# Two-slot self-attention: small copies on ScalarE, the norms of two slots together, half products and row sums in another order

## The chip, the core and the metric

One core of a Trainium2 chip runs the kernel. Its engines are TensorE (PE: matmuls; PEld: its weight loads), VectorE (DVE), ScalarE (ACT), GpSimd (POOL) and SyncE (SP), which here only issues transfers. Each engine works through its own queue in order and waits on semaphores for the others. The metric is the time of the whole program on the device, in microseconds (us); lower is better. The profile is one execution under the hardware profiler.

## What is computed

A decoder block in float32 on `x` of shape (8, 224, 512): self-attention, cross-attention against a context of 750 tokens, and a quantised feed-forward part, each followed by a residual add and a layernorm. The change touches the self-attention alone:

```python
x = _rmsnorm(tokens, norm_w)
q = x @ Wq
k, v = jnp.split(x @ Wkv, 2, axis=-1)
q = _head_rmsnorm(q, q_gamma)       # 16 heads of 64
k = _head_rmsnorm(k, k_gamma)       # x / max(norm, 1e-12) * (gamma + 1) * 8
sim = jnp.einsum('bhid,bhjd->bhij', q, k)
sim = jnp.tanh(sim / 50.0) * 50.0 * 64 ** -0.5
attn = jax.nn.softmax(sim, axis=-1)
out = jnp.einsum('bhij,bhjd->bhid', attn, v)
x = _layernorm(tokens + merge_heads(out) @ Wo)
```

## The kernel before

**Slots and groups.** Two batches `u` and two heads `j` form one *slot*. Four pairs of batches (groups 0 to 3) times eight pairs of heads (`hp` 0 to 7) make 32 slots, `m` = 0 to 31, `g, hp = divmod(m, 8)`. The order of every compute engine's instructions is the order of the program text (a manual schedule); only SP's transfers are placed by the framework.

**One slot.** `self_scores(m)` multiplies keys and queries on PE into `sc_a` (16 matmuls); ACT takes tanh and then exp into `pr`, with keys on the partitions. `self_values(m)` multiplies `pr` with the values (16 matmuls into `ov_a`), and DVE scales by the inverse row sums `rc_a` into `oT`. A slot's values are computed one slot later, in slot m + 1. In even groups POOL copies the end of `oT` into `oT_tail`. `inverse_sums(m)` makes `rc_a`: DVE transposes and adds 32 by 32 blocks of `pr` (L508, into `sm_q`), three copies bring the four quarters of the partitions together (L517), L521 adds them, two reciprocals follow (L527), three copies spread the result (L531), and two transposes broadcast it (L538).

**Two slots' queries and keys.** In an even slot `project_pair` computes queries and keys of slots m + 2 and m + 3 by a scheme with seven half products instead of eight. Each is eight matmuls and goes into one of two PSUM tiles, `mx` and `mz`, where they accumulate: ACT copies `mx` away after each of its products, DVE adds `mz` to the copy after each of its own (`add`, L397). A tile may be written again only when that copy or add has read it. The function is a generator: its yields place its parts between the other work of the slot. ACT squares the results (L393, `sq_qk`).

**Norms.** `head_norms` is called in odd slots for the two next slots, one after the other: DVE adds the squares in 32 by 32 blocks (L428, `nm_q`), four copies fetch the other half of each head (L435, `nm_o`), then an add, a maximum (L438, L439), and on POOL the power -0.5 (`rsqrt`, L129, into `nm_i`). `scale_qk` (L446, L451) transposes the inverse norms over the old squares and scales queries and keys with them; `self_scores` needs this.

**What else a slot carries.** `project_v` multiplies a tile of 128 tokens with the value weights (8 matmuls of 512 columns, copied to `v` by ACT, L471); in groups 0 to 2 `transpose_xn` and `copy_xn` turn the next group's normalised tokens, which `scale_x` (L254) makes in the slot before; `square` and `rms_norms` prepare these in slots with `hp` = 0. `self_output` multiplies a finished tile of the group before with `Wo` (16 matmuls of 512 columns, or pairs over half of the rows), in the slots that `out_at` lists, and adds it to `x` on DVE (L588); the layernorm of that tile is started in the next slot (`layernorm`, with its power on POOL) and its scaling (L152) runs at that slot's end. PSUM has three shared tiles for `mx`, `mz`, values, transposes and outputs, two for scores and one for `ov_a`.

Of the kernel before, what the change touches and what calls it, by code (L numbers as in the profile page):

```python
# [38 lines left out]
P = 128  # L39
# [23 lines left out]
def decoder_block(ctx: ExitStack, tc: tile.TileContext, a: dict, out: bass.AP):  # L63
# [153 lines left out]
    with tc.tile_pool(name="a_sb", bufs=2) as sb, tc.tile_pool(  # L217
# [16 lines left out]
        trs, mms, loaded = {}, {}, {}  # L234
        xn, qk, sq_qk, inv, v, oT, rcs = {}, {}, {}, {}, {}, {}, {}
# [35 lines left out]
        def open_qk(m):  # L271

            qk[m] = sb.tile([P, 2, 2, S], F32, name="qk", bufs=4)
            sq_qk[m] = sb.tile([P, 2, 2, S], F32, name="sq_qk")
# [5 lines left out]
        def block_qk(m, w, cols):  # L280
# [3 lines left out]
            if (w, c0) == (0, 0):  # L284
                open_qk(m)
# [79 lines left out]
        def project_pair(j):  # L365
# [4 lines left out]
            open_qk(m + 1)  # L370
# [3 lines left out]
            yield  # L374
# [27 lines left out]
            product(mz, True, 1, b21)  # L402
            add(m, 0)
            yield
            product(mx, False, 4, t2)
            nc.scalar.copy(qk[m][:, 1], mx)
            square_qk(m, 0)
            product(mz, True, 3, t1)
            product(mx, False, 5, t3)
            nc.scalar.copy(qk[m + 1][:, 1], mx)  # L410
            yield
            add(m + 1, 1)
            yield
# [9 lines left out]
        def head_norms(m):  # L423
# [3 lines left out]
            quarter = sb.tile([P, 4 * NB], F32, name="nm_q")  # L427
            nc.vector.tensor_reduce(  # L428
                quarter, sq_qk[m].rearrange("p u w (b c) -> p (u w b) c", c=Q32), AX.X,
                ALU.add, apply_transpose=True,  # L430
            )
            other = sb.tile([P, 4 * NB], F32, name="nm_o", bufs=1)
            for q in range(P // Q32):
                o = q ^ 1
                nc.vector.tensor_copy(  # L435
                    other[q * Q32 : (q + 1) * Q32], quarter[o * Q32 : (o + 1) * Q32]
                )
            nc.vector.tensor_tensor(quarter, quarter, other, ALU.add)  # L438
            nc.vector.tensor_scalar(quarter, quarter, 1e-24, None, ALU.max)  # L439
            inv[m] = sb.tile([P, 2, 2 * NB, 1], F32, name="nm_i")  # L440
            rsqrt(inv[m].rearrange("p u b o -> p (u b o)"), quarter)
# [14 lines left out]
        def project_v(i, c):  # L456

            mm = ps_mm.tile([P, 512], F32, tag="mm", name="mm_v")
# [9 lines left out]
            for b, kt, row, at, n in key_pieces(i):  # L468
                if (b, c) not in v:
                    v[b, c] = sb.tile([P, NT, 512], F32, name="v", bufs=6)  # L470
                nc.scalar.copy(v[b, c][row : row + n, kt, :], mm[at : at + n, :])  # L471
# [31 lines left out]
        def inverse_sums(m):  # L503


            quarter = sb.tile([P, 2, 2, NB, NT, P // Q32], F32, name="sm_q", bufs=1)
            for u in range(2):
# [4 lines left out]
                )  # L512

# [848 lines left out]
```

## Time and profile before

| | us |
|---|---|
| runs of the kernel, median of 3 | 1715.62 (1715.25 to 1716.76) |
| profiled execution, whole | 1714.79 |
| its span, first to last instruction | 1713.0 |
| first scores of the self-attention | 46.7 |
| last values of the self-attention | 521.2 |
| first matmul of the cross-attention's keys | 541.2 |

Durations in the self-attention, mean or median of one instruction, as the groups and tiles of the trace show them:

| instruction | ns |
|---|---|
| L508, row sums of a batch, DVE | 1089 |
| L428, norms of a slot, DVE | 1103 |
| L435 copy of 32 x 28, DVE | 210 (167 to 1083) |
| L517 copy of 32 x 56, DVE | 232 (203 to 1084) |
| L531 copy of 32 x 14, DVE | 167 |
| L438 add, L439 maximum, 128 x 28, DVE | 204, 180 |
| L129 power on 128 x 28, POOL | 4797 |
| L446 transpose, L451 scaling, 128 x 448, DVE | 619, 734 |
| L397 add, L559 `oT`, 128 x 448, DVE | 623, 619 |
| L493 tanh, L499 exp, 128 x 448, ACT | 537, 575 |
| L401 copy of `mx`, L393 square, 128 x 448, ACT | 531, 583 |

A row of the timeline gives the start, the time until the last of the merged instructions ended, the engine, the line, the operation and the tiles; in brackets how long the engine was idle before it and what released it. In a table of stretches each engine has its busy time and, in brackets, its instructions. Matmuls overlap, so a row of eight is longer than the distance to the next row; the distance is what counts.

### The profile page before, as it was taken

The numbers are of one execution on the slowest core, as the hardware profiler recorded it, in microseconds if no ns is written. First come the engines' busy times: TensorE is split into PE (matmuls) and PEld (weight loads), VectorE is DVE, ScalarE is ACT, GpSimd is POOL, SyncE is SP. The second block draws the span as 40 slices with busy tenths as digits, with TensorE's granted clock in tenths as the row PEclk, the third lists the DMA queues.
The fourth block names the chain that finished last, engine by engine and source line by source line (L and its number), as shares of the span: only waits on it lengthen the run. The fifth ranks groups of instructions, "written<-read, shape, count | busy, mean of one in ns | idle before, by whom it ended". The sixth has DMA issues, their size and how long they took to land.

```text
span 1713.0 us, 24297 instructions
## 1 busy us (share of the span) xinstructions
PE 1669.5 (97%) x8962; PEld 1150.1 (67%) x8962; DVE 1291.0 (75%) x2833; ACT 871.9 (51%) x1492; POOL 661.0 (39%) x543
## 2 busy tenths in 40 slices
PE   8999999998989999999999999999999999999998
PEld 5666666675745777776776776777776776774443
DVE  3797888777883776776886886797875776886877
ACT  3555536444531665554564565565443543445663
POOL 3562442432420444344344244344443343443244
PEclk9999999999999999999999999999999999999999
DMA  7143112111212122201121121100000000031434
GB/s 258 50 135 106 43 56 74 53 55 66 93 64 104 58 74 94 74 25 65 44 68 64 44 68 65 38 19 34 1 26 6 4 24 6 1 142 28 76 82 105
DMA packets 85573, 106.72 MB, mean 62 GB/s; under 512 B 38352, under 2 KB 58832, under 8 KB 82512
## 3 DMA queue, kind: packets, MB, share of 16 engines
q1 hardware_dynamic: 85456, 105.19, 19.4%
q8 instruction: 70, 1.15, 0.3%
q14 instruction: 47, 0.39, 0.1%
HBM read 82.36 MB, written 14.16 MB: 56 GB/s over the span
## 4 chain that ended last, share of the span: by engine, by line
PE 87%; DVE 11%; DMA 1%; issue 1%; ACT 0%; POOL 0%; POOLq 0%; SPq 0%; DVEq 0%
PE mm_k L897 15%; PE mm_v L885 15%; PE sc_c L934 9%; PE ov_c L1028 9%; PE mm_q L910 6%; PE mm_co L194 6%; PE mm_f L1163 5%; PE mm_o L579 5%; PE mm_x L383 4%; PE mm_z L383 4%; PE mm_v L461 3%; PE sc_a L483 2%; PE dn L1251 2%; DVE sm_q L508 2%; PE ov_a L551 2%; DVE nm_q L428 1%
## 5 line engine op out<-in xcount | busy, mean ns | idle before, releaser
L1018 POOL TENSOR_TENSOR csh<-cpT 125x672 f32<-125x672 f32 x128 | 207.3, 1619 | 578.8 <-DVE cpT L1008 536.8
L1016 ACT ACTIVATE cpT<-cpT 125x1344 f32<-125x1344 f32 x128 | 169.5, 1325 | 228.6 <-DVE cpT L1008 219.8
L897 PE MATMUL mm_k<-cT,xattn_Wk 128*128 128x375 f32 x768 | 258.6, 486 | 1.7 <-DMA cT<-ctxT 1.7
L885 PE MATMUL mm_v<-xattn_Wv,cT 128*125 128x256 f32 x1152 | 259.1, 379 | 0.0
L885 PEld LDWEIGHTS mm_v<-xattn_Wv,cT 128*125 128x125 f32 x1152 | 216.2, 188 | 28.9
L942 ACT COPY cpT<-sc_c 125x448 f32<-125x448 f32 x384 | 173.7, 560 | 104.3 <-PE sc_c L934 104.2
L897 PEld LDWEIGHTS mm_k<-cT,xattn_Wk 128*128 128x128 f32 x768 | 140.0, 189 | 101.6 <-issue 12.5
L1008 DVE TENSOR_TENSOR cpT<-cpT,mx_b 125x1344 f32<-125x1344 f32 x128 | 193.2, 1550 | 2.2
L129 POOL TENSOR_TENSOR nm_i<-nm_q,mhalf 128x28 f32<-128x28 f32 x32 | 153.0, 4807 | 100.9 <-DVE nm_q L439 100.9
L944 DVE TENSOR_TENSOR cm<-sc_c,cpT 125x448 f32<-125x448 f32 x128 | 74.0, 620 | 146.8 <-ACT cpT L942 146.8
L934 PE MATMUL sc_c<-cqT,ckT 64*125 64x224 f32 x1536 | 163.0, 358 | 0.0
L1028 PE MATMUL ov_c<-cpT,cv 125*64 125x224 f32 x1536 | 159.4, 357 | 0.0
L934 PEld LDWEIGHTS sc_c<-cqT,ckT 64*125 64x125 f32 x1536 | 140.3, 184 | 24.7 <-ACT ckT L904 15.0
L1028 PEld LDWEIGHTS ov_c<-cpT,cv 125*64 125x64 f32 x1536 | 104.6, 137 | 47.3 <-issue 18.2
L904 ACT COPY ckT<-mm_k 128x375 f32<-128x375 f32 x128 | 59.2, 462 | 126.5 <-PE mm_k L897 126.5
L910 PEld LDWEIGHTS mm_q<-xT,xattn_Wq 128*128 128x128 f32 x512 | 96.7, 189 | 16.3
L910 PE MATMUL mm_q<-xT,xattn_Wq 128*128 128x224 f32 x512 | 107.1, 352 | 0.0
L461 PE MATMUL mm_v<-wv,xnT 128*128 128x512 f32 x224 | 101.4, 597 | 0.0
L1163 PE MATMUL mm_f<-ternary,xqT 128*128 128x512 bf16 x448 | 98.7, 379 | 0.9 <-DVE x L1055 0.9
L579 PE MATMUL mm_o<-attn_Wo,oT 128*128 128x512 f32 (+1 forms) x224 | 99.2, 596 | 0.0
L194 PE MATMUL mm_co<-xattn_Wo,coT 128*128 128x512 f32 (+1 forms) x256 | 98.1, 594 | 0.0
L1019 POOL TENSOR_TENSOR csm<-csh 125x224 f32<-125x224 f32 x128 | 93.8, 732 | 10.0
(187 smaller groups left out, 2658.6 us busy)
## 6 DMA issues: line engine op xcount, KB each, us to landing
w_pair<-w_sums_all SPq DMA_DIRECT2D x24, 512.0 KB, 4.3
cT<-ctxT SPq DMA_DIRECT2D x8, 1125.0 KB, 5.6
w_stage<-w_gateT SPq DMA_DIRECT2D x8, 1024.0 KB, 5.2
w_stage<-w_upT SPq DMA_DIRECT2D x8, 1024.0 KB, 5.2
w_stage<-w_downT SPq DMA_DIRECT2D x8, 1024.0 KB, 5.3
tern<-w_t SPq DMA_DIRECT2D x24, 256.0 KB, 2.1
ternary<-tern SPq DMA_DIRECT2D x3, 2048.0 KB, 12.4
w_pair<-attn_Wq SPq DMA_DIRECT2D x36, 128.0 KB, 2.3
```

The source lines that it names most:

```text
L194: nc.tensor.matmul(mm[row : row + m, :], lhsT=oT[:, k, at : at + m], rhs=w[:, k, :], start=(k == 0), stop=(k == NPAIR - 1),)
L579: nc.tensor.matmul(mm[row : row + lhsT.shape[-1], :], lhsT=lhsT, rhs=wo[:, hp, :], start=(hp == 0), stop=(hp == NPAIR - 1),)
L885: nc.tensor.matmul(mm[:, i, :], lhsT=cT[:, k, c * CT : (c + 1) * CT], rhs=xwv[:, k, g * VN : (g + 1) * VN], start=(k == 0), stop=(k == KC ...
L897: nc.tensor.matmul(mm, lhsT=xwk[:, k, hp * P : (hp + 1) * P], rhs=cT[:, k, c * HALF : (c + 1) * HALF], start=(k == 0), stop=(k == KC - 1),)
L910: nc.tensor.matmul(mm, lhsT=xwq[:, k, hp * P : (hp + 1) * P], rhs=xT[:, k, :], start=(k == 0), stop=(k == KD - 1),)
L934: nc.tensor.matmul(sc[j][:, i, :], lhsT=kT[h0 : h0 + DH, ct * CT : (ct + 1) * CT], rhs=qT[h0 : h0 + DH, :], start=True, stop=True,)
L942: nc.scalar.copy(pT[:, j, 2 * c2 : 2 * c2 + 2, :], sc[j])
L1008: nc.vector.tensor_tensor(pT[:, j], pT[:, j], nm[:CT, j] .rearrange("p (o q) -> p o q", o=1) .to_broadcast([CT, NCT, S]), ALU.add,)
L1016: nc.scalar.activation(pT[:, j], pT[:, j], AF.Exp)
L1018: nc.gpsimd.tensor_tensor(half, pT[:, j, 0:3], pT[:, j, 3:6], ALU.add)
L1028: nc.tensor.matmul(ov[h0 : h0 + DH, :], lhsT=v[:, ct, hq * DH : (hq + 1) * DH], rhs=pT[:, j, ct, :], start=(ct == 0), stop=(ct == NCT - 1),)
L1163: nc.tensor.matmul(mm, lhsT=xqTs[i][:, k, :], rhs=w[:, k, cols], start=(k == 0), stop=(k == KD - 1),)
```

## The change

Four things change, all in the self-attention:

- The small copies of norms (L435) and row sums (L517, L531) move from DVE to ACT; the add and the maximum of the norms (L438, L439) move to POOL. The two reciprocals L527 become one.
- The squares of two slots lie in one tile, `sq_pair`, and `head_norms` takes both slots at once (only at the start one at a time). It is now a generator: reduction and copies stand at the end of the even slot, after that slot's own squares; POOL's part stands in the odd slot after `self_values`, ahead of that slot's layernorm.
- `inverse_sums` is a generator too: the reduction stays at the end of its slot; its later parts stand there as well in an even slot (but for the last transposes, which stand ahead of the next `self_values`), and in the next slot, between the parts of `project_pair`, after an odd one.
- The order on PE: the third half product moves ahead of `self_values`; the product with `t1` moves behind `self_scores`; `transpose_xn` moves ahead of `project_v`. In even slots the copy of the values and `copy_xn` come after the sums. Group 3 makes the outputs of group 2 in slots with `hp` 5, 6, 7 instead of 4, 5, 6, and `oT` has 15 buffers instead of 14.

```diff
...
+        sq_pair = sb.tile([P, 2, 2, 2, S], F32, name="sq_qk", bufs=1)
...
         def open_qk(m):
-            qk[m] = sb.tile([P, 2, 2, S], F32, name="qk", bufs=4)
-            sq_qk[m] = sb.tile([P, 2, 2, S], F32, name="sq_qk")
+            for i in range(2):
+                qk[m + i] = sb.tile([P, 2, 2, S], F32, name="qk", bufs=4)
+                sq_qk[m + i] = sq_pair[:, i]
...
             open_qk(m)
-            open_qk(m + 1)
             w = blocks(j)
             b11, _, b21, b22 = input_blocks(j // (NPAIR // 2))
             t1, t2, t3, t4 = (sums_x[:, i] for i in range(4))
-            yield
             mx = ps_mm.tile([P, 2, S], F32, tag="mm", name="mm_x")
             mz = ps_mm.tile([P, 2, S], F32, tag="mm", name="mm_z")
...
             product(mx, True, 0, b11)
             nc.scalar.copy(qk[m][:, 0], mx)
             product(mz, True, 1, b21)
+            yield
             add(m, 0)
             yield
             product(mx, False, 4, t2)
             nc.scalar.copy(qk[m][:, 1], mx)
+            yield
             square_qk(m, 0)
-            product(mz, True, 3, t1)
+            yield
             product(mx, False, 5, t3)
             nc.scalar.copy(qk[m + 1][:, 1], mx)
             yield
+            product(mz, True, 3, t1)
             add(m + 1, 1)
-            yield
             product(mx, False, 2, t4)
             nc.scalar.copy(qk[m + 1][:, 0], mx)
             square_qk(m + 1, 1)
...
             square_qk(m, 1)
             yield
-        def head_norms(m):
-            quarter = sb.tile([P, 4 * NB], F32, name="nm_q")
+        def head_norms(m, i0, i1):
+            quarter = sb.tile([P, 2, 4 * NB], F32, name="nm_q")[:, i0:i1]
+            quarter = quarter.rearrange("p n b -> p (n b)")
             nc.vector.tensor_reduce(
-                quarter, sq_qk[m].rearrange("p u w (b c) -> p (u w b) c", c=Q32), AX.X,
-                ALU.add, apply_transpose=True,
-            )
-            other = sb.tile([P, 4 * NB], F32, name="nm_o", bufs=1)
+                quarter,
+                sq_pair[:, i0:i1].rearrange("p n u w (b c) -> p (n u w b) c", c=Q32),
+                AX.X, ALU.add, apply_transpose=True,
+            )
+            yield
+            other = sb.tile([P, 2, 4 * NB], F32, name="nm_o", bufs=1)[:, i0:i1]
+            other = other.rearrange("p n b -> p (n b)")
             for q in range(P // Q32):
                 o = q ^ 1
-                nc.vector.tensor_copy(
+                nc.scalar.copy(
                     other[q * Q32 : (q + 1) * Q32], quarter[o * Q32 : (o + 1) * Q32]
                 )
-            nc.vector.tensor_tensor(quarter, quarter, other, ALU.add)
-            nc.vector.tensor_scalar(quarter, quarter, 1e-24, None, ALU.max)
-            inv[m] = sb.tile([P, 2, 2 * NB, 1], F32, name="nm_i")
-            rsqrt(inv[m].rearrange("p u b o -> p (u b o)"), quarter)
+            yield
+            nc.gpsimd.tensor_tensor(quarter, quarter, other, ALU.add)
+            nc.gpsimd.tensor_scalar(quarter, quarter, 1e-24, None, ALU.max)
+            for i in range(i0, i1):
+                inv[m + i] = sb.tile([P, 2, 2 * NB, 1], F32, name="nm_i")
+                at = (i - i0) * 4 * NB
+                rsqrt(
+                    inv[m + i].rearrange("p u b o -> p (u b o)"),
+                    quarter[:, at : at + 4 * NB],
+                )
+            yield
         def scale_qk(m):
             rb, r = sq_qk.pop(m), inv.pop(m)
...
                 )
         def project_v(i, c):
             mm = ps_mm.tile([P, 512], F32, tag="mm", name="mm_v")
             at = i * P % (2 * G)
...
                     start=(k == 0),
                     stop=(k == KD - 1),
                 )
-            for b, kt, row, at, n in key_pieces(i):
-                if (b, c) not in v:
-                    v[b, c] = sb.tile([P, NT, 512], F32, name="v", bufs=6)
-                nc.scalar.copy(v[b, c][row : row + n, kt, :], mm[at : at + n, :])
+            def copy_v():
+                for b, kt, row, at, n in key_pieces(i):
+                    if (b, c) not in v:
+                        v[b, c] = sb.tile([P, NT, 512], F32, name="v", bufs=6)
+                    nc.scalar.copy(v[b, c][row : row + n, kt, :], mm[at : at + n, :])
+            return copy_v
         def self_scores(m):
...
         def inverse_sums(m):
             quarter = sb.tile([P, 2, 2, NB, NT, P // Q32], F32, name="sm_q", bufs=1)
             for u in range(2):
                 nc.vector.tensor_reduce(
...
                     prs[u].rearrange("p j t (b c) -> p j t b c", c=Q32),
                     AX.X, ALU.add, apply_transpose=True,
                 )
+            yield
             flat = quarter.rearrange("p u j b t g -> p (u j b t) g")
             for g in range(1, P // Q32):
-                nc.vector.tensor_copy(
-                    flat[:Q32, :, g], flat[g * Q32 : (g + 1) * Q32, :, 0]
-                )
+                nc.scalar.copy(flat[:Q32, :, g], flat[g * Q32 : (g + 1) * Q32, :, 0])
+            yield
             tot = sb.tile([Q32, 2, 2, NB], F32, name="sm_t", bufs=1)
             nc.vector.tensor_reduce(
                 tot.rearrange("p u j b -> p (u j b)"),
                 quarter[:Q32].rearrange("p u j b t g -> p (u j b) (t g)"), AX.X, ALU.add,
             )
             isum = sb.tile([P, 2, 2 * NB, 1], F32, name="sm_i", bufs=1)
-            for j in range(2):
-                nc.vector.reciprocal(
-                    isum[:Q32, j, :, 0].rearrange("p (u b) -> p u b", u=2), tot[:, :, j]
-                )
+            nc.vector.reciprocal(
+                isum[:Q32, :, :, 0].rearrange("p j (u b) -> p j u b", u=2),
+                tot.rearrange("p u j b -> p j u b"),
+            )
+            yield
             for g in range(1, P // Q32):
-                nc.vector.tensor_copy(
+                nc.scalar.copy(
                     isum[g * Q32 : (g + 1) * Q32, g // 2, :, 0],
                     isum[:Q32, g // 2, :, 0],
                 )
+            yield
             rcs[m] = sb.tile([P, 2, S], F32, name="rc_a", bufs=1)
             for j in range(2):
                 half = slice(j * DH, (j + 1) * DH)
...
                     rcs[m][half].rearrange("p u q -> p (u q)"),
                     isum[half, j].to_broadcast([DH, 2 * NB, Q32]),
                 )
+            yield
         def self_values(m):
             g, hp = divmod(m, NPAIR)
...
                             start=(kt == 0),
                             stop=(kt == NT - 1),
                         )
-            oT[m] = sb.tile([P, 2, S], F32, name="oT", bufs=14)
+            oT[m] = sb.tile([P, 2, S], F32, name="oT", bufs=15)
             nc.vector.tensor_tensor(oT[m], ov[:, :, :S], rcs.pop(m), ALU.mult)
             if g % 2 == 0:
...
+        open_qk(0)
...
         nc.vector.tensor_scalar(gscale, gam, 1.0, DH**0.5, ALU.add, ALU.mult)
-        head_norms(0)
-        project_v(0, 0)
-        project_v(1, 0)
+        for _ in head_norms(0, 0, 1):
+            pass
+        project_v(0, 0)()
+        project_v(1, 0)()
         project_qk(1)
         sum_input(0, nc.vector)
         scale_qk(0)
         sum_weights(1, nc.vector)
-        head_norms(1)
+        for _ in head_norms(0, 1, 2):
+            pass
         for i in opened[0][2:]:
-            project_v(i, 0)
-        out_at = [(), (1, 3, 5), (1, 3, 5, 6), (4, 5, 6)]
+            project_v(i, 0)()
+        out_at = [(), (1, 3, 5), (1, 3, 5, 6), (5, 6, 7)]
+        nothing = iter(lambda: None, 0)
+        sums = norms = nothing
         for m in range(NS):
             g, hp = divmod(m, NPAIR)
             even = m % 2 == 0
-            pair = project_pair(m // 2 + 1) if even and m + 2 < NS else None
-            step = (lambda: next(pair)) if pair else (lambda: None)
-            step()
-            step()
-            if even and m > 0:
-                scale_qk(m)
+            c = 1 - hp // 4
+            tiles = opened[g + hp // 4] if g + hp // 4 < NG else ()
+            ahead = opened[g + 1] if g + 1 < NG else ()
+            turned = ahead[hp - 1] if 1 <= hp < 1 + len(ahead) else None
+            pair = nothing
+            if even and m + 2 < NS:
+                pair = project_pair(m // 2 + 1)
+            if even:
+                next(pair)
+                next(sums)
+                if m > 0:
+                    scale_qk(m)
+                next(pair)
+                next(sums)
+                next(pair)
+                next(sums)
+                next(pair)
+            next(sums)
             if m > 0:
                 self_values(m - 1)
-            step()
+            next(norms)
+            next(pair)
             self_scores(m)
             for i in due:
                 scales.append(layernorm([i]))
             due.clear()
             if even:
                 scale_qk(m + 1)
-            elif m + 1 < NS:
-                head_norms(m + 1)
-                head_norms(m + 2)
-            step()
-            step()
-            inverse_sums(m)
-            c = 1 - hp // 4
-            tiles = opened[g + hp // 4] if g + hp // 4 < NG else ()
+            next(pair)
+            if turned is not None:
+                transpose_xn(turned)
+                if not even:
+                    copy_xn(turned)
+            copy_v = lambda: None
             if hp % 4 < len(tiles):
-                project_v(tiles[hp % 4], c)
+                copy_v = project_v(tiles[hp % 4], c)
+            if not even:
+                copy_v()
+            sums = inverse_sums(m)
+            next(sums)
+            norms = nothing
+            if even:
+                if pair is not nothing:
+                    norms = head_norms(m + 2, 0, 2)
+                next(norms)
+                next(sums)
+                copy_v()
+                next(norms)
+                next(sums)
+                next(sums)
+                if turned is not None:
+                    copy_xn(turned)
             for f in scales:
                 f()
             scales.clear()
-            ahead = opened[g + 1] if g + 1 < NG else ()
-            if 1 <= hp < 1 + len(ahead):
-                transpose_xn(ahead[hp - 1])
-                copy_xn(ahead[hp - 1])
             if hp in out_at[g]:
...
         last = closed[NG - 1]
         for i in last[:2]:
             self_output(NG - 1, i, 0, NPAIR - 1)
+        for _ in sums:
+            pass
         self_values(NS - 1)
         for i in last[:2]:
             self_output(NG - 1, i, NPAIR - 1)
```

More of the change, by code (lines that the diff above doesn't have):

```diff
@@ L283, in block_qk @@
             c0, c1 = cols
-            if (w, c0) == (0, 0):
-                open_qk(m)
             if c0 == 0:
```

## The prediction

> **What bounds the kernel now.** I read the page first (span, engines), then busy time by group of eight slots, then TensorE's timeline through the self-attention for the places where it stops, then VectorE's timeline at one of those.
>
> ```profile
> span 1713.0 us, 24297 instructions
> PE 1669.5 (97%) x8962; PEld 1150.1 (67%) x8962; DVE 1291.0 (75%) x2833; ACT 871.9 (51%) x1492; POOL 661.0 (39%) x543
> ...
> 46.50:163.00 116.50, 106.14 (x568) 77.37 (x567) 97.63 (x217) 62.40 (x129) 63.52 (x45) 0.96 0.28 96
> 163.00:280.00 117.00, 114.08 (x572) 78.00 (x571) 94.52 (x224) 60.09 (x124) 44.68 (x16) 1.00 0.20 64
> 280.00:397.00 117.00, 117.00 (x578) 76.92 (x578) 88.06 (x204) 55.90 (x115) 38.12 (x22) 1.00 0.19 59
> 397.00:525.00 128.00, 114.68 (x571) 74.16 (x568) 100.57 (x243) 50.72 (x106) 40.86 (x14) 0.96 0.20 67
> ```
>
> After the stretch and its length come busy PE, weight loads, DVE, ACT, POOL, then the granted clock and DMA. The rows are roughly groups 0 to 3. Groups 1 and 2 are full; 0 and 3 have idle PE, a lower clock, and a DVE busy for 84% and 79%. All that the change touches lies before 525 us, so only PE's lost time there can be won.
>
> TensorE, then VectorE, around slot 28:
>
> ```profile
> 455.97 1.78 PE L383 MATMUL mm_x<-x_sums,w_pair 128*128 128x224 f32 x8
> 461.60 3.23 PE L383 MATMUL mm_z<-x_sums,w_pair 128*128 128x224 f32 x8 [3.85 <-DVE qk L397]
> 464.67 1.68 PE L383 MATMUL mm_x<-x_sums,w_pair 128*128 128x224 f32 x8
> ...
> 451.02 1.10 DVE L428 TRANSPOSE_TENSOR_REDUCE nm_q<-sq_qk 128x28 f32<-128x896 f32 x1
> 453.22 1.10 DVE L428 TRANSPOSE_TENSOR_REDUCE nm_q<-sq_qk 128x28 f32<-128x896 f32 x1
> 455.43 2.10 DVE L508 TRANSPOSE_TENSOR_REDUCE sm_q<-pr 128x28 f32<-128x896 f32 x2
> 457.56 0.64 DVE L517 COPY sm_q<-sm_q 32x56 f32<-32x56 f32 x3
> 459.58 1.31 DVE L538 STREAM_TRANSPOSE rc_a<-sm_i 64x448 f32<-64x448 f32 x2
> 460.92 0.62 DVE L397 TENSOR_TENSOR qk<-mm_z,qk 128x448 f32<-128x448 f32 x1
> ```
>
> Eight half-product matmuls normally start 1.51 us after the last eight. Here the gap is 5.63, because `mz` may not be overwritten before the add L397, which stands behind 9.9 us of norms and row sums on DVE. The next eight take 3.07: after the stop PE runs slowly for a while.
>
> I take start minus start, minus the regular length (1.51 for eight half-product matmuls, 1.71 scores, 1.67 values, 3.44 a value tile, 6.87 an output tile), and add what exceeds 0.25 us. Group 0 loses 17.2 (from 67.86: 3.0+1.6; 124.22: 3.0+0.4+1.5; 150.30: 4.1+0.3+1.6; four small ones 1.7), group 1 nothing, group 2 3.4 (212.52: 2.3; 276.63: 1.1), group 3 19.5 (402.80: 4.6+0.6+1.3; 433.89: 0.7; 455.97: 4.1+1.6; 488.53: 4.8+1.3+0.5). Together 40.1 us: nothing in this change can win more.
>
> One more place matters, in slot 9, the transposes of the next group's first tile:
>
> ```profile
> 172.59 3.70 PE L461 MATMUL mm_v<-wv,xnT 128*128 128x512 f32 x8
> ...
> 174.69 0.72 ACT L254 ACTIVATE xn<-x,rms_rs 128x512 f32<-128x512 f32 x1 [1.32 <-POOL rms_rs L129]
> ...
> 176.13 0.60 PE L262 MATMUL tr_x<-ident,xn 128*128 128x128 f32 x4
> ```
>
> Its input `xn` is done at 175.41, only just before the transposes; the value tile ahead of them hides that.
>
> **What the Trainium skill says.** "ScalarE: Activation LUTs", section "What ACT_TABLE_LOAD costs": an instruction with immediate operands takes 186 ns plus 0.833 ns a column, and neighbours overlap by 93 ns. The trace agrees: 448 columns would be 559 ns, its rows have 531 (L401) to 583 (L393). "TensorE: Matmul & The Clock Gate", "Part 1": an idle PE falls to half clock and returns after sustained work; the trace shows it (3.07 instead of 1.51 after 3.85 idle). "Perfetto Trace Analysis", "Optimization Strategy": find what blocks the gaps and make it start sooner; that is how I go on.
>
> **The change, part by part.** *DVE relief.* In 46 to 525 us DVE loses the copies L435 (25.2), L517 (22.3), L531 (16.0), the operations L438 and L439 (11.5) and half of L527 (5.3): 80 us of 381. The two norm reductions become one of twice the width; no row has it, but L508's two take 2.10 and they cannot do less than the work of L428, so 2.1.
>
> *ACT load.* Ten copies a pair for norms and per slot six for sums: about 250 copies. None is in the trace; by the skill a 28-column one lasts 0.21 and follows after 0.12. I take 0.16 per copy within its chain (four 0.65, three 0.5). Bounds: 0.12 (all overlap) and 0.30 (each waits its own hand-over). ACT rises from 48% to about 56%; what counts is that its queue is in order.
>
> *POOL.* Add and max on 56 columns: nearest `oT_tail` with 64 columns, 0.24; I take 0.25 each (0.15 to 0.5). The two powers stay 4.79 each.
>
> *The cycle.* Let T be the end of the seventh half product of an even slot, P1 the start of the first of the next pair. The add ends T+0.65, row sums T+2.75, norms T+4.85, their four copies T+5.5, the three `isum` copies T+6.1. POOL gives the first inverse norm at T+5.5+0.5+4.8 = T+10.8. In groups 0 and 2 POOL's `oT_tail` copy stands in front, and waits for `oT` (T+6.1+1.3+0.6): T+13.6. From that inverse to the seventh product DVE needs scale 2.4, add 0.6, sums 0.7, ACT copies 0.5, transposes 1.3, `oT` 0.6, scale 2.4, add 0.6 = 9.1. Undisturbed, the seventh starts at P1+12.4, so the inverse must be there at P1+3.3. P1 is T+10.3 where both slots have a value tile, T+17.2 with an output in the odd slot (all pairs in the middle of groups 1 and 2: no wait), T+6.9 without a value tile in the odd slot. The stops of the kernel before on L397 go, and these are late next:
> - *Transposes moved ahead of the value tile* (odd slots). In slot 9 the squares now follow the norm and sum copies on ACT: T+6.1, four squares 3.0, mean and POOL 1.2, `xn` 0.7: T+11.1. Scores end at T+6.8, so PE waits 4.3; three squares in groups 0 and 2: 3.3 and 3.4. In groups 1 and 2 the slow clock adds 1.5 each (as at 124.22), in group 0 the next wait absorbs it. Slots 3, 11, 19 wait 0.5 to 0.8.
> - *Group 0*: POOL reaches the norms of slots 2 and 3 only after its delayed mean and eight weight sums (5.8), so scores(2) wait 1.4 and the seventh product 1.9; slot 8 has P1 at T+6.9 and the inverse at P1+6.7: 3.4; in slot 0 two `mx` products stand together: 0.7. With the transposes (3.3 and 0.8) 11.5.
> - *Slots 23 and 24*: the layernorm's power now stands behind both norm powers on POOL, and DVE's L152 waits for it ahead of `scale_qk(24)`. Inverses at P1+4.9 and +9.7, L152 done at +10.9, the seventh product at 10.9+9.1 = +20.0: 7.6 late (before: 6.5).
> - *Rest of group 3*: slot 28 has P1 at T+6.9 and no tail: 1.2; scores(30) wait 2.8 for DVE, whose output add stands in front.
>
> Free edits: the startup norms (ACT idle for 2.29 us before L471's first copies), one more `oT` buffer, the output moved within group 3, the deferred last sums (12.4 us of output matmuls cover them). SP's loads keep their order; `w_pair` lands 4.3 us after issue, over 10 us ahead of use.
>
> Sum of lost PE time after: group 0 11.5, group 1 4.3+1.5+0.5 = 6.3, group 2 3.4+1.5+0.5 = 5.4, group 3 7.6+1.2+2.8 = 11.6: 34.8. Against 40.1: 5.3 less. The profiled execution took 1714.79 (1.8 around its span), so 1709.5; the median shown is 0.8 higher, so **1710**.
>
> **Rivals.** *A, the norm waits vanish too*: if hand-overs are quicker than I count and inverses come in time, only the waits for `xn` remain (4.8 in group 0, 6.3, 5.4 = 16.5): 23.6 less, 1692. For it: the 80 us taken from DVE. Against: POOL's two powers of 4.79 are untouched. *B, ACT's queue becomes the bound*, slower: 7 copies are in each of three `xn` waits (and four in part at slots 3, 11, 19), 7 to 10 in each of six inverse-to-seventh chains, so 0.1 us more per copy costs about 9.5 us. From 0.22 us per copy the gain is gone; at 0.28 it is 11.4 - 5.3 = 6 slower, 1722. For it: every copy waits for another engine and holds up exponentials and `mx` copies. Against: DVE's own such copies follow after 0.18. *C, an exact trade*: the stops of groups 0 and 3 just change their name, 1714.
>
> **Numbers.** Forecast 0.50, A 0.18, B 0.18, C 0.14. What can be told from no change is 0.2%, 3.4 us: 1712.2 to 1719.0. The forecast's own range is 1703 to 1716 (POOL and copy prices), of which 0.36 is faster, 0.13 same, 0.01 slower; A gives 0.18 faster; C 0.03, 0.08, 0.03; B 0.01 same and 0.17 slower: 0.57, 0.22, 0.21. The range takes the near half of A and B: 1691 to 1721.
>
> **What would show it.** Right: PE's stops on L397 in groups 0 and 3 gone; in slots 1, 9, 17 a stop of 3 to 5 us with `tr_x` released by `xn` on ACT; near slot 24 a DVE wait for `ln_rs`; group 1 longer than before, group 3 shorter by about 8. Wrong: small ACT copies above 0.22 us, `mx` products that wait for ACT in the middle of groups 1 and 2, or no stop at the transposes.

## The result and the profile after

The changed kernel takes 1727.72 us, the median of four runs (1723.86 to 1728.52), against 1715.43 us for the kernel before beside it. The ratio is 1.0067, 95% interval 1.0049 to 1.0084. A second series, run later beside the kernel before, gave 1725.42 and 1.0057 (1.0043 to 1.0071). So the change is slower by 9 to 12 us, where 5 us less had been forecast. The profiled execution took 1727.02 us, with a span of 1725.2 against 1713.0.

The head of the page after (span, then busy time, share and number of instructions of each engine):

```profile
span 1725.2 us, 24169 instructions
...
PE 1671.9 (97%) x8962; PEld 1148.8 (67%) x8962; DVE 1210.7 (70%) x2402; ACT 938.7 (54%) x1752; POOL 671.7 (39%) x577
```

The load moved as the change meant it to: VectorE lost 80 us and ScalarE took over 67, and yet the span grew by 12.2. The loss must therefore be in the waits of TensorE. I compare the start of the same work in the two traces (self-attention scores of a slot, then the first keys of cross-attention), in us:

| start of | before | after | difference |
|---|---|---|---|
| scores, slot 0 | 46.71 | 45.88 | -0.8 |
| scores, slot 8 | 160.84 | 155.43 | -5.4 |
| scores, slot 10 | 192.96 | 196.64 | +3.7 |
| scores, slot 16 | 282.45 | 284.72 | +2.3 |
| scores, slot 18 | 314.92 | 323.88 | +9.0 |
| scores, slot 24 | 413.81 | 426.04 | +12.2 |
| scores, slot 28 | 466.27 | 476.15 | +9.9 |
| first mm_k of cross-attention | 541.19 | 549.26 | +8.1 |
| second mm_k | 552.93 | 565.00 | +12.1 |
| end of span | 1712.98 | 1725.21 | +12.2 |

Group 0 did win 5 us. Slots 8 to 10, 16 to 18 and 18 to 24 lost 19 us, and 4 us were lost where cross-attention begins, outside everything that the forecast looked at. From there on the difference is constant.

What TensorE waited for between 46 and 540 us, in the kernel after (total us, times, longest):

```profile
PE tr_x L264 <- ACT xn L256: 16.4, 6, 4.7
PE sc_a L500 <- DVE qk L463: 8.3, 4, 5.0
PE mm_z L382 <- DVE qk L396: 4.8, 3, 2.4
PE mm_x L382 <- ACT qk L400: 4.0, 4, 1.8
```

In the kernel before, the first place was held by `mz` waiting for the add on VectorE, 19.3 us in eight stops. That wait is down to 4.8, and slot 28, shown of before with a stop of 4.1 us, now reads like this on TensorE (start, us of the group, tile and count; in brackets the idle time ahead and what ended it):

```profile
467.61 1.68 PE L382 MATMUL mm_z<-xnT,w_pair 128*128 128x224 f32 x8
471.06 1.78 PE L382 MATMUL mm_x<-x_sums,w_pair 128*128 128x224 f32 x8 [1.78 <-ACT qk L400]
```

and on VectorE:

```profile
461.84 2.00 DVE L430 TRANSPOSE_TENSOR_REDUCE nm_q<-sq_qk 128x56 f32<-128x1792 f32 x1
```

The norms of both slots are one reduction, long past when the products come. A smaller stop, 1.9 us, is left on a ScalarE copy. So the mechanism that the change was made for works. What replaced it stands in three other places.

**The transposes.** Slot 9 after, on TensorE (the forecast showed the same place of before):

```profile
168.56 1.78 PE L500 MATMUL sc_a<-qk 64*128 64x224 f32 x16
175.06 1.12 PE L264 MATMUL tr_x<-ident,xn 128*128 128x128 f32 x4 [4.73 <-ACT xn L256]
175.97 5.95 PE L474 MATMUL mm_v<-wv,xnT 128*128 128x512 f32 x8
```

and on ScalarE:

```profile
168.35 0.98 ACT L440 COPY nm_o<-nm_q 32x56 f32<-32x56 f32 x4
169.34 0.62 ACT L550 COPY sm_i<-sm_i 32x14 f32<-32x14 f32 x3
169.99 0.63 ACT L245 ACTIVATE sq_x<-x 128x512 f32<-128x512 f32 x1
...
174.29 0.72 ACT L256 ACTIVATE xn<-x,rms_rs 128x512 f32<-128x512 f32 x1 [1.32 <-POOL rms_rs L129]
```

The scores take 6.50 us to the next start instead of 1.71. The value tile that could have filled the gap stands behind the transposes, and it then takes 5.95 us instead of 3.60: the granted clock, 1.00 until 173.9 us, is 0.50 from there for 6.8 us. Slots 1 and 17 stop for 3.75 us each and lose another 2.6 and 2.7; slots 3, 11 and 19 lose 1.5 each. Together that is 25 us.

**GpSimd's queue**, its timeline near slots 18 and 24:

```profile
315.48 0.24 POOL L585 COPY oT_tail<-oT 128x64 f32<-128x64 f32 x1 [14.55 <-PE mm_o L600]
...
316.50 9.56 POOL L129 TENSOR_TENSOR nm_i<-nm_q,mhalf 128x28 f32<-128x28 f32 x2
...
411.82 0.24 POOL L585 COPY oT_tail<-oT 128x64 f32<-128x64 f32 x1 [18.37 <-DVE oT L580]
...
422.37 0.55 POOL L129 TENSOR_TENSOR ln_rs<-ln_ve,mhalf 128x1 f32<-128x1 f32 x1
```

A 0.24 us copy of `oT`'s tail stands ahead of the norms. In slots 3, 5, 7, 19 and 21 it holds them up for 2.55 us. Near slot 24 it waits 18.4 us for VectorE, while the norms' input has been ready since 405.8 (four copies of L440 from 404.79, 0.97 long): the norms start 6.3 us late. The two powers behind the copy take 9.6 us, and the layernorm's power, for which VectorE waits 6.4 us, comes last. Near slot 18 the copy waits 14.6 us for TensorE, and the norms, ready at 296.9, start 18.8 us late.

**The start of cross-attention**, on TensorE:

```profile
561.57 3.50 PE L985 MATMUL sc_c<-cqT,ckT 64*125 64x224 f32 x24 [2.96 <-DVE cqT L969]
```

and on VectorE:

```profile
561.04 0.38 DVE L969 TENSOR_SCALAR cqT<-mm_q 128x224 f32<-128x224 f32 x1
```

The first query copy ends 12.2 us after the first mm_k; in the kernel before it was 9.0. After, five layernorms are left for the end of self-attention instead of four, each a round from VectorE to GpSimd and back of 2.27 us, and the query copy stands behind all five.

### The profile page after: what moved, and what is told of

Its sections match the earlier page's. It is cut to its first block, busy times and chain, and to the rows that moved or that the text cites. A ratio compares the mean times of both kernels' runs of the same rounds, so it can differ in the third digit from the quotient of the medians.

```text
span 1725.2 us, 24169 instructions
## 1 busy us (share of the span) xinstructions
PE 1671.9 (97%) x8962; PEld 1148.8 (67%) x8962; DVE 1210.7 (70%) x2402; ACT 938.7 (54%) x1752; POOL 671.7 (39%) x577
## 4 chain that ended last, share of the span: by engine, by line
PE 87%; DVE 5%; ACT 3%; POOL 2%; issue 1%; DMA 1%; SPq 0%; POOLq 0%; DVEq 0%; ACTq 0%
PE mm_k L948 15%; PE mm_v L936 14%; PE sc_c L985 9%; PE ov_c L1079 9%; PE mm_co L194 6%; PE mm_q L961 6%; PE mm_f L1214 5%; PE mm_o L600 5%; PE mm_v L474 4%; PE mm_x L382 4%; PE mm_z L382 3%; PE dn L1302 2%; PE sc_a L500 2%; PE ov_a L572 2%; POOL nm_i L129 1%
## 5 line engine op out<-in xcount | busy, mean ns | idle before, releaser
L474 PE MATMUL mm_v<-wv,xnT 128*128 128x512 f32 x224 | 107.5, 627 | 0.0
```

Of the source, the lines that this page charges most:

```text
L474: nc.tensor.matmul(mm, lhsT=xnT[:, k, at : at + P], rhs=wv[:, k, c * 512 : (c + 1) * 512], start=(k == 0), stop=(k == KD - 1),)
```

## The experiments

Each edit is made on the changed kernel unless said otherwise. Ratios are to the kernel before, measured beside it.

| | edit | us | ratio, 95% interval |
|---|---|---|---|
| E1 | transposes behind the value tile | 1711.85 | 0.9976 (0.9967 to 0.9985) |
| E2 | outputs of group 3 in slots 4, 5, 6 | 1723.20 | 1.0038 (1.0027 to 1.0049) |
| E3 | norms ahead of the tail on GpSimd | 1710.88 | 0.9977 (0.9970 to 0.9985) |
| E4 | small copies on VectorE | 1723.47 | 1.0044 (1.0031 to 1.0056) |
| E5 | E1 + E2 + E3 | 1694.36 | 0.9876 (0.9861 to 0.9891) |
| E6 | E5, small copies on VectorE | 1692.89 | 0.9869 (0.9853 to 0.9884) |
| E7 | kernel before, transposes ahead | 1719.20 | 1.0020 (1.0013 to 1.0027) |
| E8 | E5, only the sums' copies on VectorE | 1695.69 | 0.9874 (0.9856 to 0.9893) |
| E9 | E5, half products in the old order | 1702.65 | 0.9919 (0.9905 to 0.9934) |
| E10 | E2, two buffers for the tails | 1717.19 | 1.0004 (0.9995 to 1.0014) |
| E11 | E9, small copies on VectorE | 1709.61 | 0.9962 (0.9949 to 0.9976) |
| E12 | none (the change again) | 1725.42 | 1.0057 (1.0043 to 1.0071) |

My theory: three placements cost the time, the transposes, the tail's copy, and the output in the last slot. The main rival: the small copies, short as they are, choke ScalarE's queue.

**E1, the transposes.**

```diff
-            if turned is not None:
-                transpose_xn(turned)
-                if not even:
-                    copy_xn(turned)
             copy_v = lambda: None
             if hp % 4 < len(tiles):
                 copy_v = project_v(tiles[hp % 4], c)
+            if turned is not None:
+                transpose_xn(turned)
+                if not even:
+                    copy_xn(turned)
             if not even:
                 copy_v()
```

> The changed kernel with one edit: the transposes of the next group's tile stand behind the value tile on TensorE again, in every slot that has them. Theory (the transposes wait for xn, whose ScalarE queue is late, and the value tile of 3.4 us no longer hides it): the stops of 4.8, 3.75 and 3.75 us in slots 9, 1 and 17 and the slow matmuls behind them (2.8, 2.6, 2.7), with 1.5 us in each of slots 3, 11 and 19, fall to under 1 us each: 25 us at most, some of it coming back as later waits for the norms, so 13 to 22 us less than the changed kernel, that is 1706 to 1715. Rival (the small ScalarE copies themselves are the cause, the transposes only show it): PE stops at the next wait instead, and under 5 us are won, 1723 to 1728.

1711.85: some 14 to 16 us less than the change's 1725.4 and 1727.7. TensorE's wait for `xn` falls from 16.4 us to 2.3. New waits take part of it back: the wait of the scores for VectorE rises from 8.3 to 10.6, that of the half products for the add from 4.8 to 6.5, and 2.2 us that the profile puts down to GpSimd are new. The theory holds, and the rival's bound of 5 us is passed.

**E2, the outputs.**

```diff
-        out_at = [(), (1, 3, 5), (1, 3, 5, 6), (5, 6, 7)]
+        out_at = [(), (1, 3, 5), (1, 3, 5, 6), (4, 5, 6)]
```

> The changed kernel with one edit: the outputs of group 3 in slots 4, 5, 6 of the group again instead of 5, 6, 7. Theory (the output in the last slot makes a fifth layernorm stand ahead of the first query of cross-attention on VectorE): the wait of sc_c for cqT (2.96 us) and about 1 us of slow matmuls behind it go, 4 us less, 1723 to 1725; the output of slot 4 may cost up to 2 of these again at slot 28. Rival (the last slot's output only fills a place that would be empty): no gain, 1727 to 1730.

In the trace the wait for `cqT` drops from 2.96 to 0.75 us, and the stretch from first to second mm_k from 15.74 to 12.57 (11.74 before the change). That is 3.2 us at the place named. The times alone don't show it: the runs range from 1718.7 to 1725.3, and the interval overlaps that of E12.

**E3, the tail.** Only GpSimd's order changes.

```diff
+            next(norms)
             if m > 0:
                 self_values(m - 1)
-            next(norms)
```

> The changed kernel with one edit: on GpSimd the norms' add, max and two powers are issued ahead of the copy of oT's tail instead of behind it. Nothing else is moved on any engine. Theory (in groups 0 and 2 the norms' input is ready some 6 us before that copy, which waits for VectorE's oT): powers start 4 to 6 us earlier in groups 0 and 2, VectorE's wait for ln_rs near slot 24 (6.4 us) and PE's stops at slot 24 (7.4 us), slot 18 (3.2) and part of those of slots 2 and 8 (1.3 and 4.5) go: 8 to 13 us less, 1714 to 1720. Rival (two powers of 4.8 us on GpSimd are the bound themselves, or the scores wait for VectorE's own queue): under 3 us.

1710.88, 15 to 17 us less, more than expected. GpSimd near slot 18, in E3:

```profile
298.26 9.57 POOL L129 TENSOR_TENSOR nm_i<-nm_q,mhalf 128x28 f32<-128x28 f32 x2
309.45 0.24 POOL L585 COPY oT_tail<-oT 128x64 f32<-128x64 f32 x1 [1.62 <-PE mm_o L600]
```

The powers begin 5.4 us after the start of slot 17's scores (292.82); after the change it was 20.2 (316.50 - 296.28). TensorE's stops at slot 18 are gone, those of slot 24 shrink from 7.4 us to about 1, and the scores' waits for VectorE from 8.3 to 3.3. Part of the gain in the profiled run is chance: the stops of slots 1 and 17 are as long as ever (3.75), but the matmuls after them lost 0.1 us each instead of 2.6 and 2.7. E12, the change itself once more, has the same, so the edit did not do it; the last section shows what did. What else lies beyond the 13 us expected was not traced.

**E4, the engine of the copies.**

```diff
-                nc.scalar.copy(
+                nc.vector.tensor_copy(
                     other[q * Q32 : (q + 1) * Q32], quarter[o * Q32 : (o + 1) * Q32]
...
-                nc.scalar.copy(flat[:Q32, :, g], flat[g * Q32 : (g + 1) * Q32, :, 0])
+                nc.vector.tensor_copy(flat[:Q32, :, g], flat[g * Q32 : (g + 1) * Q32, :, 0])
...
-                nc.scalar.copy(
+                nc.vector.tensor_copy(
                     isum[g * Q32 : (g + 1) * Q32, g // 2, :, 0],
```

> The changed kernel with one edit: the small copies of norms and sums (four, three and three of them) on VectorE again, at the same places of the order. Theory (order, not the engine of the copies, is what costs): the stops at the transposes stay, shorter by at most the 1 to 2 us that ScalarE's queue wins, while VectorE carries some 60 us more and delays the adds: the time stays within 5 us of the changed kernel, 1723 to 1733. Rival (copies on ScalarE with their hand-overs of 0.2 to 0.3 us cause the loss): at least 8 us less, 1720 or below.

1723.47: at the near edge of the theory's band and above the rival's 1720 or below. The copies do lengthen the `xn` waits: without them the stop of slot 9 is 2.9 us instead of 4.8, those of slots 1 and 17 2.6 instead of 3.75, and slots 3, 11 and 19 stop no longer (wait for `xn` 7.9 us in all, instead of 16.4). But VectorE gives it back: waits for the add rise from 4.8 to 9.0, the scores' waits from 8.3 to 13.5. So E4 shows that the choice of the engine nets 2 to 4 us, not that the copies are free on ScalarE.

**E5 and E6, all three, and the copies once more.** E5 holds the three diffs above, E6 adds that of E4.

> The changed kernel with the three edits together: transposes behind the value tile, outputs of group 3 in slots 4, 5, 6, norms ahead of the tail's copy on GpSimd. Alone they gave 16, 4.5 and 17 us. Theory (three separate places): they add up, less what two of them share in slots 9 and 17: 1687 to 1697. Rival (the stops replace one another, one resource sets the pace): no more than 7 us below the best single edit, 1704 or above.

> The three edits together, with the small copies on VectorE again. Theory (with the order mended, the VectorE relief is worth something, since the seventh half product, the row sums and the scaling all hang on VectorE's queue): 4 to 12 us more than the three edits alone, 1692 to 1707. Rival (the engine of the small copies does not matter, order is all): within 3 us of the three edits together.

E5 is 21 us faster than the kernel before and 31 to 33 faster than the change: the three edits add up to 33 of the 37 us that they gave one by one (16 + 17 + 4.5, against the first series; against the second it is 31 of 30). In E6 the theory loses. I expected VectorE's relief to be worth 4 to 12 us, but the copies on VectorE cost nothing (1692.89 against 1694.36, intervals overlapping). What TensorE waits for most, first in E5, then in E6:

```profile
PE mm_x L382 <- ACT qk L400: 6.2, 5, 2.2
PE sc_a L500 <- DVE qk L463: 3.7, 2, 2.1
PE mm_z L382 <- DVE qk L396: 2.7, 2, 2.3
```

```profile
PE mm_z L382 <- DVE qk L396: 6.7, 5, 2.7
PE sc_a L500 <- DVE qk L463: 4.4, 2, 2.6
```

The rival's bound of 3 us holds. It is nearly an even trade: with ScalarE's copies the third product waits for the `mx` copy on ScalarE, with VectorE's the seventh waits for the add.

**E7, the transposes alone**, in the kernel before: `transpose_xn` and `copy_xn` are taken from the slot's end and put ahead of `project_v`.

> The kernel before with one edit: the transposes of the next group's tile, and the copy after them, stand ahead of the value tile. All small copies are still on VectorE and the sums still in one piece. Theory (xn is late in itself, in slot 9 at about 3 us after the scores' end, and the value tile hid it): new stops at tr_x of 2 to 3 us in slots 1, 9 and 17 with slow matmuls behind, 4 to 12 us more than before, 1720 to 1728. Rival (only the copies queued on ScalarE ahead of xn make the stop): within 3 us of before.

1719.20, 3.7 us more than before, just under the theory's band and above the rival's. Slots 1, 9 and 17 stop for 1.4, 2.9 and 1.4 us. So the new place costs something even with nothing added to ScalarE's queue, but in slots 1 and 17 more than half of the 3.75 us comes with the rest of the change. E4, with the small copies off ScalarE, had 2.6, 2.9 and 2.6: in slot 9 all of the excess over E7 is the copies'; in slots 1 and 17 half of it is, and the other half was not traced further.

**E8, E9 and E11: which part of the change pays.** E8 puts only L536 and L550 back on VectorE. E9 is E5 with the old order of half products, E11 also has E4's edit:

```diff
             product(mz, True, 1, b21)
-            yield
             add(m, 0)
-            yield
+            for _ in range(4):
+                yield
             product(mx, False, 4, t2)
             nc.scalar.copy(qk[m][:, 1], mx)
-            yield
             square_qk(m, 0)
-            yield
+            product(mz, True, 3, t1)
             product(mx, False, 5, t3)
             nc.scalar.copy(qk[m + 1][:, 1], mx)
             yield
-            product(mz, True, 3, t1)
             add(m + 1, 1)
```

> The three edits together, with the six small copies of the row sums on VectorE again and the norms' four still on ScalarE. Theory (the sums' copies on ScalarE wait for VectorE's reduction and hold back the value copies, the exponentials and the next mx copy behind them, where PE stops 6.2 us for L400; the norms' copies cost VectorE the time that E6 loses at L396): both stops shrink, 1 to 4 us less than the three edits alone, 1690 to 1693. Rival (small copies are of no account on either engine): within 1 us of 1694.

> The three edits together, with the half products in the order of the kernel before: the first add ahead of the scaling on VectorE, the third, fourth and fifth product together behind the values. Theory (the new order pays by leaving the fourth product, on mz, to wait less for the first add): the stops of mz for L396 of 2 to 4 us return in slots 2, 6, 8, 24 and 28 and the stops for L400 (6.2 us) go: 3 to 12 us more than the three edits alone, 1697 to 1706. Rival (the joint norms alone bring the gain): within 3 us of the three edits together, or less.

> The three edits together, with the half products in the order of the kernel before and the small copies on VectorE: of the change, the joint norms, the sums in steps and GpSimd's add and max are left. Theory (with the sums' copies on ScalarE the fifth product waits for the mx copy behind them, 12.7 us in eight stops; with the copies on VectorE that goes, and the old order of products does no harm): 8 to 13 us below the 1702.7 us of the old order with ScalarE's copies, 1689 to 1695. Rival (the order of the half products is what pays, whichever engine copies): VectorE's added copies bring the stops of mz for L396 back, 1699 to 1706.

E8 is a miss: 1695.69, no gain, the rival's band within its spread. E9 costs 8.3 us, as expected in size, but not for the reason I gave: the waits for the add did not return. In E9, and then in E11, the largest wait of TensorE is

```profile
PE mm_x L382 <- ACT qk L406: 12.7, 8, 5.8
```

```profile
PE mm_z L382 <- DVE qk L396: 20.1, 14, 3.7
```

In E9 the fifth product needs the copy of the third, and that stands on ScalarE behind the `isum` copies, which wait for VectorE. So I expected in E11 that VectorE's copies would mend it. They made it worse by 7 us: the old wait for the add is back at 20 us, now in 14 stops instead of 8. The rival named the right wait, though the time lies 3.6 us above even its band. Set side by side, as ratios to the kernel before:

| | copies on ScalarE | copies on VectorE |
|---|---|---|
| new order of half products | 0.9876 (E5) | 0.9869 (E6) |
| old order | 0.9919 (E9) | 0.9962 (E11) |

The new order is worth 0.4% to 0.9%. ScalarE's copies are worth 0.4% with the old order, and nothing with the new one. What E11 itself still has over the kernel before, 0.4%, belongs to what is left of the change (joint norms ahead of the tail, GpSimd's add and max, sums in steps, the later copies in even slots, one more `oT` buffer) together; these were not separated.

**E10, why the tail waits near slot 18.** The tails have one buffer. The first tail of group 2 may not overwrite group 0's while an output tile of group 1 still reads it. `oT` goes back to 14 buffers to make room.

```diff
-                    tails[g] = sb.tile([P, NPAIR, TAIL], F32, name="oT_tail", bufs=1)
+                    tails[g] = sb.tile([P, NPAIR, TAIL], F32, name="oT_tail", bufs=2)
...
-            oT[m] = sb.tile([P, 2, S], F32, name="oT", bufs=15)
+            oT[m] = sb.tile([P, 2, S], F32, name="oT", bufs=14)
```

> The changed kernel with the outputs of group 3 in slots 4, 5, 6 again (which alone measured 1723.2 us), and two buffers for the copies of oT's tail instead of one, with oT's own down from 15 to 14 to make room. GpSimd's order is left as the change has it. Theory (near slot 18 the first tail copy of group 2 waits 14.6 us for the output tile that still reads group 0's tails from the only buffer, and the norms stand behind it): that wait and PE's stops of slot 18 (3.2 us) and part of the slow matmuls and waits that follow them go, 3 to 7 us less than 1723.2, while the stop of 5.2 us near slot 24, where the tail waits for VectorE, stays: 1716 to 1720. Rival (near slot 18 too the tail waits for VectorE's oT, the buffer is free in time): 1721 to 1725.

GpSimd near slot 18 in E10:

```profile
301.47 0.24 POOL L585 COPY oT_tail<-oT 128x64 f32<-128x64 f32 x1 [1.05 <-DVE oT L580]
...
302.48 9.56 POOL L129 TENSOR_TENSOR nm_i<-nm_q,mhalf 128x28 f32<-128x28 f32 x2
```

1717.19 against E2's 1723.20, with intervals clear of each other. The wait of 14.6 us is gone, TensorE's stops at slot 18 (0.6 and 2.6) as well, and the stop of 5.2 us at slot 24 stands unchanged, because there the tail waits for VectorE. Part of the 6 us is beyond these stops: the profiled executions of E10 and E2 differ by only 2.3 us.

**E12, the change again.**

> The changed kernel as it is, on the chip and beside the kernel before of the last run, because its four runs ranged over 4.7 us and the smallest single edit (outputs in slots 4, 5, 6) brought only 4.5. If the first result is typical: a ratio between 1.005 and 1.0084 again, 1724 to 1729, and the outputs' edit (1.0038) is clear of it. If it lies at 1.004 or below, that edit was not shown to gain anything by its time.

1725.42, in the range. E2's interval is not clear of it, so for E2 I rely on the trace.

## Why the prediction was wrong

It forecast 1710 from 34.8 us of lost TensorE time; the trace has 49.4, and 4.0 more at the start of cross-attention. Two steps failed. Two waits in other engines' queues were put at nothing, for the output moved within group 3 (4.0 us) and for the pair of slot 18 (3.2). And the term for the transposes, with the slow matmuls and slots 3, 11 and 19, was too small: 15.8 us forecast, 24.9 measured here and 19.4 in the trace of E12. By the prediction's own terms, in us (measured is what exceeds the regular length by over 0.25, in the profiled run after):

| term | predicted | measured |
|---|---|---|
| waits for `xn`, slots 1, 9, 17 | 3.3 + 4.3 + 3.4 | 3.75 + 4.80 + 3.75 |
| slow matmuls after these | 0 + 1.5 + 1.5 | 2.6 + 2.8 + 2.7 |
| slots 3, 11, 19 | 0.8 + 0.5 + 0.5 | 1.5 + 1.5 + 1.5 |
| rest of group 0 | 7.4 | 7.1 |
| slot 16 | 0 | 0.4 |
| slot 18 | 0 | 3.2 |
| slot 24 | 7.6 | 7.4 |
| slots 28, 30 and the end | 4.0 | 6.3 |
| sum | 34.8 | 49.4 |
| start of cross-attention | 0 | 4.0 |

Before, 40.1 were lost; 53.4 would make the span 13.3 longer, and it is 12.2 longer, as slot 0 starts 0.8 earlier.

- *The mechanism at the transposes was right, its size wrong.* Place, releaser and length of the stops in slots 1, 9 and 17 came out within 0.5 us. Slots 3, 11 and 19 were 2.7 low in sum. The copies are the reason: E4 removes these stops altogether. I had taken 0.16 us per copy in its chain; the price was 0.20 to 0.29 (below). (The prediction speaks of ten copies a pair for the norms; there are four, and its 250 copies count four.) The slow matmuls behind the stops, 3.0 against 8.1, are in good part chance: in E12 they took 0.1, 2.4 and 0.1 us. In slot 1 the next waits do absorb them, as forecast: from the scores of slot 1 to those of slot 3 both traces take 33.32 us, with 2.6 us of slow matmuls and 1.3 of later stops in the one and 0.1 and 4.0 in the other.
- *"The output moved within group 3" at nothing was wrong.* I checked that TensorE had other work, and not what stands ahead of the next stage's first instruction on VectorE: one more layernorm, 2.27 us, and 4.0 with the slow matmuls after the stop. E2 shows 3.2 of it.
- *"All pairs in the middle of groups 1 and 2: no wait" failed at slot 18.* I had the tail's copy ahead of the norms, but let it wait for `oT` only, 2.8 us in the cycle (2.55 measured in the other pairs). It also waits for its one buffer, here 14.6 us, and E10 shows that this buffer is the cause of the 3.2.
- *Slot 24 was right by luck* (7.6 against 7.4): I put the cause into the order of the layernorm's power behind the norms'. E3 left that order and moved only the tail, and 6.5 of the 7.4 us went. The tail holding up the norms was the link to look at: I had named it for the cycle, at 2.8 us, and it held them up for 6.3.
- *The rest of group 0* was somewhat low: 7.4 us forecast against 9.7, counting the slow matmuls of slot 1, which only take the place of its later stops. The stops on L397 of before did go, and the joint reduction took 2.00 us for 2.1.
- *Rival B* stood within 6 us of the result, but by another mechanism. It made the copies' price the point of decision, with over 11 us from them at 0.28. The mean price, 0.24 in the run after, is above its threshold of 0.22 and would by its 9.5 us per 0.1 cost an estimated 8 us. With the copies off ScalarE (E4), 2 to 4 us were won, and none with the order mended (E6). *Rival A*'s gain of 23.6 was nearly there to be had, in E5 and E6 (21 and 23 us), but not by quicker hand-overs: the powers had to start earlier, and the waits for `xn`, which A kept, had to go too.

## What to carry to other kernels

When a change moves a step, ask of each engine's queue what now stands behind it, up to the first instruction of the next stage. A tiny copy at the head of an in-order queue, here 0.24 us of `oT` tail, can cost more than a change is to win (15 to 17 us in E3), when it waits for a buffer or another engine and slow work stands behind it. And a tile of independent work belongs between a late producer and its consumer: moving 3.4 us of matmuls from ahead of the transposes to behind them cost 14 to 16 us here (E1), and 3.7 in the kernel before (E7).

## What the runs showed of the hardware

**The clock is set anew every 3.41 us.** In ten profiled runs, stops of TensorE of 4.1 to 6.0 us in self-attention (19 of them) always cost 1.4 to 3.1 us more in the next two groups of matmuls. Of those between 1.8 and 3 us, 34 of 42 cost 0.0 to 0.2, the other eight 0.9 to 1.9. And the same stop of 3.75 us, in slots 1 and 17, cost 2.6 and 2.7 in the run after, 1.8 and 1.8 in E10, and 0.1 each in E3 and in E12. The length alone does not decide.

The trace's records of the granted clock do. They show 1.00 or 0.50 only. In each of the 14 traces all falls lie on a grid of 3.413 us, within 0.002 us: in the run after at 61.23, 173.87, 300.16 and 426.46 us, 33, 37 and 37 steps apart. For every step between 46 and 525 us I added up TensorE's idle time (with the ends of matmuls as the profile models them). After all 41 steps at full clock with 2.07 us of idle time or more, the next step has half the clock; after none of the 1844 with up to 1.95; in between, after three of nine. Half clock goes on for a second step where the first has 0.80 us of idle time or more (12 of 12), and ends where it has up to 0.52 (32 of 32).

So what a stop costs depends on how it falls on the grid. The stop in slot 1 puts 2.01 us of idle time into one step and 1.66 into the next in the run after, and 1.85 and 1.83 in E12. A stop of over 4 us always leaves some 2 us in one step, wherever it falls; a stop just under 4 us can go either way, which makes a kernel's times scatter. E12's profiled run was 3.0 us shorter than that of the first series, and 2.6 of that lie between the scores of slots 17 and 18 (25.03 us against 27.60).

**Small copies on ScalarE.** Mean ns of one, in the run after (total busy us first, then the mean, then idle time ahead):

```profile
L536 ACT COPY sm_q<-sm_q 32x56 f32<-32x56 f32 x96 | 28.2, 294 | 30.6 <-DVE sm_q L526 29.6
L550 ACT COPY sm_i<-sm_i 32x14 f32<-32x14 f32 x96 | 19.2, 200 | 34.6 <-DVE sm_i L544 33.0
L440 ACT COPY nm_o<-nm_q 32x56 f32<-32x56 f32 x60 | 14.1, 235 | 3.2 <-DVE nm_q L430 2.5
L444 POOL TENSOR_TENSOR nm_q<-nm_q,nm_o 128x56 f32<-128x56 f32 x15 | 4.5, 301 | 63.0 <-ACT nm_o L440 63.0
```

The Trainium skill ("ScalarE: Activation LUTs", "What ACT_TABLE_LOAD costs") gives 186 ns plus 0.833 ns a column; for 14 and 56 columns that is an estimate of 198 and 233 ns, and L550 and L440 agree. L536, which reads and writes every fourth element, takes 60 ns more than L440; that the stride is the cause was not tested. The overlap of 93 ns between neighbours, on which my 0.16 rested, did not appear in these chains: four L440 took 0.98 us, 0.24 each, where two activations of 448 columns (L392, 0.58 alone) took 1.04. GpSimd's add on 56 columns took 0.30, for 0.25 assumed.
